# Head 0's first evictions by another engine, padded quarters, another order of the first two products, and two more products of zeros, in a two-layer graph attention kernel

## The chip, the cores and the metric

The kernel runs on one core of a Trainium2 chip. The time is that of the device, in microseconds, of one execution of the whole program. The engines have these names in the profile: PE is TensorE (PEld its weight loads), DVE is VectorE, ACT is ScalarE, POOL is GpSimd, SP is SyncE, which mostly issues DMAs. Each of them takes its instructions in order from a queue of its own and waits for the others by semaphores.

## The reference

A graph of 512 nodes has 16896 directed edges, sorted by destination: two times 8192 drawn ones and a loop at each node. Two layers of graph attention follow each other, the first with 8 heads, the second with one; all widths are 768. Then comes a residual and a layer norm.

```python
def gat_layer(x, W, a_s, a_d, b, edge_index, concat):
    n = x.shape[0]
    H, C = a_s.shape
    h = (x @ W).reshape(n, H, C)
    src, dst = (edge_index[0], edge_index[1])
    alpha_s = jnp.einsum('nhc,hc->nh', h, a_s)
    alpha_d = jnp.einsum('nhc,hc->nh', h, a_d)
    e = jax.nn.leaky_relu(alpha_s[src] + alpha_d[dst], NEG_SLOPE)
    m = jax.ops.segment_max(e, dst, num_segments=n)
    e = jnp.exp(e - m[dst])
    denom = jax.ops.segment_sum(e, dst, num_segments=n)
    alpha = e / (denom[dst] + EPS)
    msg = h[src] * alpha[:, :, None]
    out = jax.ops.segment_sum(msg, dst, num_segments=n)
    out = out.reshape(n, H * C) if concat else out.mean(axis=1)
    return out + b
h = jax.nn.elu(gat_layer(x, W1, a_src1, a_dst1, b1, edge_list, concat=True))
out = gat_layer(h, W2, a_src2, a_dst2, b2, edge_list, concat=True)
y = _layernorm(x + out)
```

## The kernel before

**Counts instead of edges.** The kernel turns the edge list into a dense matrix of counts, `cnt` (512 x 512: how many edges lead from a source to a destination), once, at the start. With it each head's attention is dense: logits for all pairs, a row maximum over existing edges, an exponential weighted by the counts, and a product with the features.

The 16896 edges are 132 chunks (`EC`) of 128 edges. For each chunk a one-hot of its sources (`os`, 128 x 512) is made, and TensorE multiplies it with a one-hot of its destinations (`od`), 32 nodes wide, and adds the product up in PSUM (L554, "counting"). Since the edges are sorted by destination, each chunk touches at most two blocks of 32 nodes, and these blocks are known in advance. `rel` (L265) is an edge's destination less the first node of either block. `destinations` (L507) compares `rel` with 0 to 31 (`offsets`) and so makes `od` for a quarter of the chunks, 33 of them, in one VectorE instruction; it rounds the quarter's bounds outwards to even columns, so that 34 columns are written. The comparisons come in the order of quarters 0, 2, 1, 3.

The one-hots of the sources are made by VectorE (L528, `is_equal`) or, for the destinations of the third quarter of nodes, by ScalarE (L526, `Sign`, from the negated index `nidx`, L611); they lie in 32 buffers that VectorE and ScalarE share in turn. Nine batches of 16 chunks (four in the last) are written out by hand: a batch makes its quarter's destinations if they are missing, its one-hots, then `extra` work, then a few of the items of the first projections (below), and then counts. `wants` says how many items are done by the end of each batch; evictions that VectorE has to do wait for the middle of the next batch's one-hots (`waiting`).

**Products by seven parts.** Each large fp32 product (512 x 768 by 768 x 768, or the aggregation) is split two by two and done with seven half-size products, P1 to P7 (a Strassen-like scheme), whose sums of operands are made by VectorE or by adding DMAs. A part has two row blocks (`i` = 0, 1) of 128 rows, and each has three contraction steps `k` of 128 (`product`, L305 to L310). The trace shows each such fp32 step as two records, so a row block is six.

`first_projection` is head 0's x times W1. Its P1 goes to two PSUM banks of the pool `held`; ScalarE copies them out (L430); later parts are added into the same banks. x is turned by TensorE (`turn_x(t, r)`, L213: three transposes of row tile t, column half r, into a bank of the pool `mm`, then a ScalarE copy to `xT`, L214). Half 0 of tiles 0 and 1 is turned ahead of everything; the rest comes between the items: `turns = {1: [(0, 1), (1, 1)], 3: [(2, 0), (3, 0), (2, 1), (3, 1)]}` says after how many items. After the first item `nidx` is made, and after each item some of the one-hots of ScalarE.

`keep_warm(n)` (L184) multiplies zeros, 128 x 128 by 128 x 512, n times, into a bank that nothing reads yet: five times at the very beginning, once after the first transposes.

**The heads.** For each head h the loop at L848 does the aggregation (`mixed`, L757, ends with ELU into `gT`), then `second`, head h's part of the second layer's projection (gT times a block of W2, added into `h2` and `u2`), with the next head's attention (`lift`, `leak`, `rank`, `weigh`) in between, and then `projection` of the head after next. In `second`, P2 is accumulated into P1's bank and P4 into P7's, P3 into P5's; between those the bank is evicted (`empty`, L362 to L367). For head 0 `h2` and `u2` are new, so the first eviction to each is a plain copy or negation by VectorE (L365); for the later heads it is an addition (L367). Around head 0's `second` the order is: both row blocks of P1; the eviction of block 0; the rest of the ELU; `gsums[0]`; the eviction of block 1; `gsums[1]`; a sum of W2; P2's blocks and the other sums; P2's evictions; then P6, P7, P4, P5, P3 with one tile of the attention beside each.

Of the kernel before, what the change touches and what calls it, by code (L numbers as in the profile page):

```python
# [8 lines left out]
F32 = mybir.dt.float32  # L9
F16 = mybir.dt.float16  # L10
BF16 = mybir.dt.bfloat16
# [3 lines left out]
ALU = mybir.AluOpType  # L15
# [21 lines left out]
def gat_pass(  # L37
# [16 lines left out]
    nc = tc.nc  # L54
# [127 lines left out]
    def keep_warm(n):  # L182
        for _ in range(n):
            nc.tensor.matmul(idle, zeros[:, :P], zeros, start=True, stop=True)  # L184

    keep_warm(5)
    nodes = ohp.tile([P, N], F16, name="nodes")
    nc.gpsimd.iota(nodes, pattern=[[1, N]], base=0, channel_multiplier=0,
                   allow_small_or_imprecise_dtypes=True)
# [30 lines left out]
    if general:  # L220
        nc.vector.tensor_copy(idx_f, idx_i)
        idx = ohp.tile([P, 2, EC], F32, name="idx")
        psi = tr.tile([P, 512], F32, name="tr")
        for j in range(2):
            for r in range(2):
                nc.tensor.transpose(psi[:, (2 * j + r) * EH:(2 * j + r + 1) * EH], idx_f[:, j, r, :],
                                    ident[:EH, :EH])
        nc.vector.tensor_copy(idx, psi[:, :2 * EC].rearrange("p (j c) -> p j c", j=2))
    else:

        B = 32
        blocks = []
        for c in range(EC):
            m = (c + 0.5) * P * N / E
            b = int(m // B)
            slack = 2 + 16 * (m / N * (1 - m / N)) ** 0.5
            lo, hi = b - (m - b * B < slack), b + ((b + 1) * B - m < slack)
            blocks.append(range(max(lo, 0), min(hi, N // B - 1) + 1))  # L240
        assert max(map(len, blocks)) <= 2


        base = ohp.tile([P, 2, EC], F32, name="base")
        for k in range(2):
            firsts = [b[k] if k < len(b) else None for b in blocks]
            lo = 0
            while lo < EC:
                hi = lo + 1
                while hi < EC and firsts[hi] == firsts[lo]:  # L250
                    hi += 1
                nc.gpsimd.memset(base[:, k, lo:hi], float(2 * N if firsts[lo] is None else firsts[lo] * B))
                lo = hi
        offsets = ohp.tile([P, B, 2, EC // NT + 1], F16, name="offsets")
        nc.vector.tensor_copy(offsets.rearrange("p b k c -> p b (k c)"),
                              nodes[:, :B].unsqueeze(2).to_broadcast([P, B, 2 * (EC // NT + 1)]))
        nc.vector.tensor_copy(idx_f, idx_i)
        turn_x(0, 0)
        turn_x(1, 0)
        psi = tr.tile([P, 512], F32, name="tr")  # L260
        for j in range(2):
            for r in range(2):
                nc.tensor.transpose(psi[:, j * EC + r * EH:j * EC + (r + 1) * EH], idx_f[:, j, r, :], ident[:EH, :EH])
        rel = ohp.tile([P, 2, EC], F16, name="rel")
        nc.vector.tensor_tensor(rel, psi[:, :EC].unsqueeze(1).to_broadcast([P, 2, EC]), base, op=ALU.subtract)  # L265
        idx = ohp.tile([P, EC], F32, name="idx")
        nc.vector.tensor_copy(idx, psi[:, EC:2 * EC])

# [83 lines left out]
    def second(h, A_, B_):  # L352

        bank = {}

        def pair(p, i, start, acc, new):
            def multiply(between=None):
                if start:
                    bank[i] = mm.tile([P, 512], F32, name="mm")
                product(bank[i], A_, B_, p, i, start, between)  # L360

            def empty():  # L362
                a, ps = acc(i), bank[i][:, :HALF]
                if new and (h == 0 or h == H - 1 and p == "P1"):
                    nc.vector.tensor_scalar(a, ps, -1.0 if p == "P7" else 1.0, None, op0=ALU.mult)  # L365
                else:
                    nc.vector.tensor_tensor(a, a, ps, op=ALU.subtract if p == "P7" else ALU.add)  # L367
            return multiply, empty

        steps = [  # L370
            ("P1", True, lambda i: u2[:, i, :], True),
            ("P2", False, lambda i: h2[:, i, L], True),
            ("P6", True, lambda i: u2[:, i, :], False),
            ("P7", True, lambda i: h2[:, 2 + i, R], True),
            ("P4", False, lambda i: h2[:, 2 + i, L], True),
            ("P5", True, lambda i: h2[:, 2 + i, R], False),
            ("P3", False, lambda i: h2[:, i, R], True),
        ]
        return [pair(p, i, *rest) for p, *rest in steps for i in range(2)]
# [29 lines left out]
        nc.vector.tensor_tensor(cnt[:, t, :], steps[:, 1:], steps[:, :N], op=ALU.subtract)  # L409
        nc.scalar.activation(absent[:, t, :], cnt[:, t, :], AF.Relu, bias=far, scale=NO_EDGE)  # L410

    def first_projection(h, XA, B_):


        HS[h] = hs = hpool.tile([P, NT, D], F32, name="hs")
        new_alpha(h)
        bank = {}

        def step(p, over, i, out, op):
            def multiply():  # L420
                if over is None:
                    bank[p, i] = (held if p == "P1" else mm).tile([P, 512], F32, name="held" if p == "P1" else "mm")
                else:
                    bank[p, i] = bank[over, i]
                product(bank[p, i], XA, B_, p, i, over is None)

            def empty():
                ps, o = bank[p, i][:, :HALF], out(i)
                if op is None:
                    nc.scalar.copy(o, ps)  # L430
                else:
                    nc.vector.tensor_tensor(o, o, ps, op=op)
            return multiply, empty, op is not None

        steps = [
            ("P1", None, lambda i: hs[:, i, L], None),
            ("P2", None, lambda i: hs[:, i, L], ALU.add),
            ("P5", None, lambda i: hs[:, 2 + i, R], None),
            ("P3", "P5", lambda i: hs[:, i, R], None),
            ("P6", "P1", lambda i: hs[:, i, R], ALU.subtract),  # L440
            ("P7", "P1", lambda i: hs[:, 2 + i, R], ALU.subtract),
            ("P4", "P1", lambda i: hs[:, 2 + i, L], None),
        ]
        return [step(p, over, i, out, op) for p, over, out, op in steps for i in range(2)]

    def spread(h):
        BC[h] = tr.tile([P, 512], F32, name="tr")
# [36 lines left out]
        nc.scalar.activation(nb1T, psb[:, :H * DC], AF.Copy, scale=-1.0)  # L484

    XA, xsums = left(xT, xS)
    items = first_projection(0, XA, B0)
    again = None
    if not general:

# [9 lines left out]
            hits[b] = hits.get(b, 0) + 1  # L500
        todo = dict(hits)
        cps, done = {}, set()
        od = ohp.tile([P, B, 2, EC], BF16, name="odw", bufs=1)

        def destinations(lo, hi):
            lo, hi = lo // 2 * 2, (hi + 1) // 2 * 2
            nc.vector.tensor_tensor(od[:, :, :, lo:hi], rel[:, :, lo:hi].unsqueeze(1).to_broadcast([P, B, 2, hi - lo]),  # L507
                                    offsets[:, :, :, :hi - lo], op=ALU.is_equal)

        def inside():  # L510

            below = ohp.tile([P, 2, EC], F16, name="below")
            nc.vector.tensor_scalar(below, rel, float(B), None, op0=ALU.is_lt)
            nc.vector.scalar_tensor_tensor(below, rel, 0.0, below, op0=ALU.is_ge, op1=ALU.mult, accum_out=found)

# [27 lines left out]
        def count(batch, rest):  # L543


            for c, b in ((c, b) for c in batch for b in blocks[c]):
                queues[b * B % P // B].append((c, b, hot[c, by_steps(b)]))
            while any(queues) and (rest or all(queues) or sum(map(len, queues)) > 3):
                for c, b, h_ in [q_.pop(0) for q_ in queues if q_]:
                    t, r = b * B // P, b * B % P  # L550
                    if t not in cps:
                        pool, name = (bc, "bc") if t == S else (tr, "tr")
                        cps[t] = pool.tile([P, 512], F32, name=name)
                    nc.tensor.matmul(cps[t][r:r + B, :N], od[:, :, b - blocks[c][0], c], h_,  # L554
                                     start=todo[b] == hits[b], stop=todo[b] == 1,
                                     tile_position=(0, r), skip_group_check=True)
                    todo[b] -= 1
            for t in range(NT):
                if t not in done and all(todo[b] == 0 for b in range(t * P // B, (t + 1) * P // B)):
                    (counted_by_steps if t == S else counted)(t, cps[t])  # L560
                    done.add(t)


        turns = {1: [(0, 1), (1, 1)], 3: [(2, 0), (3, 0), (2, 1), (3, 1)]}
        keep_warm(1)
        found = const.tile([P, 1], F32, name="found")
        wholes = len(items)
# [17 lines left out]
        pos, made, quarter, waiting = 0, set(), EC // NT, []  # L585
        for n, batch in enumerate(batches):
            for k in sorted({c // quarter for c in batch} - made):
                destinations(k * quarter, (k + 1) * quarter)
                made.add(k)
            sources(kinds(batch, False), waiting)  # L590
            ahead = kinds(batches[n + 1], True) if n + 1 < len(batches) else []
# [522 lines left out]
```

## Time and profile before

| | |
|---|---|
| three runs | 647.89, 647.94, 646.70 us (median 647.89) |
| the profiled execution | 647.22 us |
| its span, first to last instruction | 645.4 us |
| granted TensorE clock, mean | 0.998 |
| PE busy | 634.1 us (98%), 2327 matmul records |
| DVE busy | 517.4 us (80%) |
| ACT busy | 280.1 us (43%) |
| POOL busy | 46.1 us (7%) |
| DMA | 100.32 MB, mean 155 GB/s |

A profile shows one execution. A timeline row has the start and the duration in us, the engine, the line of the kernel, the operation, what it writes and reads, its shape and the number of instructions merged into the row; in brackets stand the idle time of the engine ahead of it and what ended that. The chain of waits is followed back from the last instruction: at each step to what released it, or to the instruction ahead of it on its engine. Busy PE is not PE at its peak, since matmuls are pipelined.

### The profile page before, as it was taken

What the parts mean: (1) busy time and instruction counts of PE and PEld (TensorE: products, weight loads), DVE (VectorE), ACT (ScalarE), POOL (GpSimd) and SP (SyncE); (2) the same over time, 40 slices, a digit from 0 to 9 for tenths busy, and PEclk for the clock granted to TensorE, in tenths of its full rate; (3) what the DMA queues carried; (4) which work ended last, traced back from release to release, by engine and by line L of the source; (5) the groups of instructions that cost most, each with busy time, mean ns of one, the idle gap of its engine ahead of it and who ended that gap; (6) DMA issues with size and microseconds to landing.
All of it is one profiled execution on the core that took longest, in us unless ns stands there. A gap on an engine that the chain in (4) does not pass through costs nothing.

```text
span 645.4 us, 7150 instructions
## 1 busy us (share of the span) xinstructions
PE 634.1 (98%) x2327; PEld 402.4 (62%) x2327; DVE 517.4 (80%) x1128; ACT 280.1 (43%) x472; POOL 46.1 (7%) x89
## 2 busy tenths in 40 slices
PE   8999999999999999999999999999999999999995
PEld 5555585556855586556855586556855586544553
DVE  8799989978689678878689678878689678876775
ACT  5865744530726035530726035530725035543440
POOL 1300011010000110011000110010000110000000
PEclk9999999999999999999999999999999999999999
DMA  8993488696715794196715794196815990410222
GB/s 297 326 230 87 74 248 270 151 256 193 188 55 135 187 257 139 27 259 187 188 56 134 188 258 138 29 258 193 185 54 139 233 258 16 107 50 0 30 60 77
DMA packets 81096, 100.32 MB, mean 155 GB/s; under 512 B 39654, under 2 KB 63006, under 8 KB 81054
## 3 DMA queue, kind: packets, MB, share of 16 engines
q1 hardware_dynamic: 67646, 78.57, 39.8%
q0 software_dynamic: 12976, 20.65, 18.4%
q10 hardware_dynamic: 432, 0.59, 0.3%
q8 instruction: 20, 0.33, 0.2%
q14 instruction: 22, 0.18, 0.1%
HBM read 86.93 MB, written 1.59 MB: 137 GB/s over the span
## 4 chain that ended last, share of the span: by engine, by line
PE 94%; DVE 4%; ACT 1%; DMA 1%; issue 0%; DVEq 0%; ACTq 0%
PE mm L309 62%; PE mm L779 20%; PE mm L725 3%; PE mm L1060 3%; PE held L309 2%; PE tr L554 1%; DVE os L528 1%; DMA hs<-in_x_dram 1%; PE mm L213 0%; PE bc L554 0%; DVE scr L318 0%; PE tr L984 0%; DVE h L365 0%; DVE q L475 0%; DVE q L470 0%
## 5 line engine op out<-in xcount | busy, mean ns | idle before, releaser
L309 PE MATMUL mm<-w,gT 128*128 128x384 f32 x288 | 96.8, 488 | 0.2 <-DVE u L365 0.2
L309 PE MATMUL mm<-w,xT 128*128 128x384 f32 x264 | 88.2, 487 | 0.0
L309 PEld LDWEIGHTS mm<-w,gT 128*128 128x128 f32 x288 | 54.3, 190 | 38.1 <-issue 1.6
L309 PEld LDWEIGHTS mm<-w,xT 128*128 128x128 f32 x264 | 49.9, 190 | 35.3 <-ACT os L526 0.8
L783 ACT COPY u<-mm 128x256 f32<-128x256 f32 x21 | 7.8, 372 | 140.5 <-PE mm L779 140.5
L477 ACT ACTIVATE q<-q,nmax 128x512 f32<-128x512 f32 x36 | 25.8, 721 | 95.4 <-DVE nmax L475 95.4
L779 PE MATMUL mm<-PT,hs 128*128 128x256 f32 x252 | 61.3, 379 | 0.0
L309 PE MATMUL mm<-w1t,gS 128*128 128x384 f32 x180 | 60.6, 486 | 0.0
L309 PE MATMUL mm<-w2t,xS 128*128 128x384 f32 x168 | 56.6, 487 | 0.0
L779 PEld LDWEIGHTS mm<-PT,hs 128*128 128x128 f32 x252 | 47.8, 190 | 8.4 <-issue 0.4
L309 PEld LDWEIGHTS mm<-w1t,gS 128*128 128x128 f32 x180 | 34.1, 190 | 24.2 <-issue 0.6
L367 DVE TENSOR_TENSOR h<-h,mm 128x384 f32<-128x384 f32 x72 | 39.1, 550 | 12.5 <-PE mm L309 12.0
L309 PEld LDWEIGHTS mm<-w2t,xS 128*128 128x128 f32 x168 | 31.8, 190 | 22.4 <-ACT q L466 0.4
L779 PE MATMUL mm<-pS,gS 128*128 128x256 f32 x168 | 43.2, 380 | 0.0
L707 ACT COPY PT<-zr 128x1024 uint16<-128x1024 uint16 x34 | 39.5, 1161 | 2.6 <-DMA zr<-pS 2.0
L779 PEld LDWEIGHTS mm<-pS,gS 128*128 128x128 f32 x168 | 31.8, 190 | 4.7 <-DVE pS L752 0.4
L702 ACT COPY pS<-q 128x1024 uint16<-128x1024 uint16 x26 | 27.2, 1045 | 16.6 <-DVE q L687 16.6
L309 PE MATMUL mm<-w1t,gT 128*128 128x384 f32 x96 | 32.4, 487 | 0.5 <-DVE h L365 0.5
L309 PE MATMUL mm<-w,gS 128*128 128x384 f32 x96 | 32.6, 486 | 0.0
L309 PE MATMUL mm<-w,xS 128*128 128x384 f32 x96 | 32.5, 487 | 0.0
L367 DVE TENSOR_TENSOR u<-u,mm 128x384 f32<-128x384 f32 x28 | 15.4, 553 | 18.8 <-PE mm L309 18.7
L108 POOL DMA_DIRECT2D w1t<-in_L_gnn_W_dram x7 | 8.9, 1267 | 302.3 <-DVE hs L742 173.5
(187 smaller groups left out, 1080.5 us busy)
## 6 DMA issues: line engine op xcount, KB each, us to landing
w<-in_L_gnn_W_dram SPq DMA_DIRECT2D x91, 384.0 KB
w<-in_L_gnn_W_dram POOLq DMA_DIRECT2D x16, 576.0 KB, 8.7
w2t<-in_L_gnn_W_dram SPq DMA_DIRECT2D x10, 576.0 KB
w1t<-in_L_gnn_W_dram SPq DMA_DIRECT2D x9, 576.0 KB
w2t<-in_L_gnn_W_dram POOLq DMA_DIRECT2D x8, 576.0 KB, 8.8
w1t<-in_L_gnn_W_dram POOLq DMA_DIRECT2D x7, 576.0 KB, 8.3
a_s<-in_L_gnn_a_src_dram SPq DMA_DIRECT2D x8, 384.0 KB
a_d<-in_L_gnn_a_dst_dram SPq DMA_DIRECT2D x8, 384.0 KB
```

Of the source, the lines that this page charges most:

```text
L108: nc.gpsimd.dma_start(t1, upper[:, :, R], accum_op=ALU.add)
L309: nc.tensor.matmul(ps[:, :HALF], A_[p][:, k, i * P:(i + 1) * P], B_[p][:, k, :], start=start and k == 0, stop=k == HK - 1, skip_group_chec ...
L367: nc.vector.tensor_tensor(a, a, ps, op=ALU.subtract if p == "P7" else ALU.add)
L477: nc.scalar.activation(q, q, AF.Exp, bias=nmax, scale=-1.0)
L528: nc.vector.tensor_scalar(o, nodes, idx[:, c:c + 1], None, op0=ALU.is_equal)
L554: nc.tensor.matmul(cps[t][r:r + B, :N], od[:, :, b - blocks[c][0], c], h_, start=todo[b] == hits[b], stop=todo[b] == 1, tile_position=(0, ...
L702: nc.scalar.copy(apart.rearrange("p (h n) -> p h n", h=2), q.bitcast(U16).rearrange("p (n h) -> p h n", h=2))
L707: nc.scalar.copy(PT.rearrange("p s n -> p (s n)").bitcast(U16).rearrange("p (s n h) -> p s n h", s=NT, h=2)[:, :, t * P:(t + 1) * P, :], p ...
L725: nc.tensor.matmul(ps[:, :N], HS[h][:, s, c * P:(c + 1) * P], PT[:, s, :], start=(s == 0), stop=(s == NT - 1))
L779: nc.tensor.matmul(bank[p][:, :HN], A_[p][:, k, c * P:(c + 1) * P], B_[p][:, k, :], start=over is None and k == 0, stop=k == 1, skip_group ...
L783: nc.scalar.copy(u, part("P1"))
L1060: nc.tensor.matmul(ps[:, :cols.stop - cols.start], PT[:, s, t * P:(t + 1) * P], h2[:, s, cols], start=(s == 2), stop=(s == 1))
```

## The change

1. `keep_warm(5)` becomes `keep_warm(7)`.
2. `rel`, `od`, `offsets` and `below` get a dimension for the quarters, each `QW` = 34 columns wide instead of sharing 132; the 34th column of `rel` is filled with -1 by GpSimd. `destinations` takes a quarter's number and writes that quarter alone.
3. In `second`, head 0's evictions of P1 and P2 are copies by ScalarE instead of multiplications by 1 on VectorE.
4. The first two items (P1 of head 0's projection, row blocks 0 and 1) become one: `firsts` does step k = 0 for both row blocks, step 1 for both, then `between()`, which turns half 1 of x's tiles 0 and 1, then step 2 for both. The second item's `multiply` does nothing; both evictions come after `firsts`, each at its old place.

```diff
-    keep_warm(5)
+    keep_warm(7)
...
+        QC = EC // NT
+        QW = QC + QC % 2
         base = ohp.tile([P, 2, EC], F32, name="base")
+        rel = ohp.tile([P, 2, NT, QW], F16, name="rel")
...
-        offsets = ohp.tile([P, B, 2, EC // NT + 1], F16, name="offsets")
+        if QW > QC:
+            nc.gpsimd.memset(rel[:, :, :, QC:], -1.0)
+        offsets = ohp.tile([P, B, 2, QW], F16, name="offsets")
...
-        rel = ohp.tile([P, 2, EC], F16, name="rel")
-        nc.vector.tensor_tensor(rel, psi[:, :EC].unsqueeze(1).to_broadcast([P, 2, EC]), base, op=ALU.subtract)
+        nc.vector.tensor_tensor(rel[:, :, :, :QC],
+                                psi[:, :EC].rearrange("p (q c) -> p q c", c=QC).unsqueeze(1).to_broadcast([P, 2, NT, QC]),
+                                base.rearrange("p k (q c) -> p k q c", c=QC), op=ALU.subtract)
...
             def empty():
                 a, ps = acc(i), bank[i][:, :HALF]
-                if new and (h == 0 or h == H - 1 and p == "P1"):
+                if new and h == 0 and p in ("P1", "P2"):
+                    nc.scalar.copy(a, ps)
+                elif new and (h == 0 or h == H - 1 and p == "P1"):
                     nc.vector.tensor_scalar(a, ps, -1.0 if p == "P7" else 1.0, None, op0=ALU.mult)
...
-    def first_projection(h, XA, B_):
+    def first_projection(h, XA, B_, between):
...
+        def firsts():
+            for k in range(HK):
+                if k == HK - 1:
+                    between()
+                for i in range(2):
+                    if k == 0:
+                        bank["P1", i] = held.tile([P, 512], F32, name="held")
+                    nc.tensor.matmul(bank["P1", i][:, :HALF], XA["P1"][:, k, i * P:(i + 1) * P], B_["P1"][:, k, :],
+                                     start=k == 0, stop=k == HK - 1, skip_group_check=True)
+
+        items = [step(p, over, i, out, op) for p, over, out, op in steps for i in range(2)]
+        for i, multiply in enumerate((firsts, lambda: None)):
+            items[i] = (multiply, *items[i][1:])
+        return items
...
+    def rest_of_x():
+        if not general:
+            for t in range(2):
+                turn_x(t, 1)
+
+    items = first_projection(0, XA, B0, rest_of_x)
...
-        od = ohp.tile([P, B, 2, EC], BF16, name="odw", bufs=1)
-
-        def destinations(lo, hi):
-            lo, hi = lo // 2 * 2, (hi + 1) // 2 * 2
-            nc.vector.tensor_tensor(od[:, :, :, lo:hi], rel[:, :, lo:hi].unsqueeze(1).to_broadcast([P, B, 2, hi - lo]),
-                                    offsets[:, :, :, :hi - lo], op=ALU.is_equal)
+        od = ohp.tile([P, B, 2, NT, QW], BF16, name="odw", bufs=1)
+
+        def destinations(q_):
+            nc.vector.tensor_tensor(od[:, :, :, q_, :], rel[:, :, q_, :].unsqueeze(1).to_broadcast([P, B, 2, QW]),
+                                    offsets, op=ALU.is_equal)
...
-        turns = {1: [(0, 1), (1, 1)], 3: [(2, 0), (3, 0), (2, 1), (3, 1)]}
+        turns = {3: [(2, 0), (3, 0), (2, 1), (3, 1)]}
```

More of the change, by code (lines that the diff above doesn't have):

```diff
@@ L253, in gat_pass @@
                 lo = hi
-        offsets = ohp.tile([P, B, 2, EC // NT + 1], F16, name="offsets")
+        if QW > QC:
+            nc.gpsimd.memset(rel[:, :, :, QC:], -1.0)
+        offsets = ohp.tile([P, B, 2, QW], F16, name="offsets")
         nc.vector.tensor_copy(offsets.rearrange("p b k c -> p b (k c)"),
-                              nodes[:, :B].unsqueeze(2).to_broadcast([P, B, 2 * (EC // NT + 1)]))
+                              nodes[:, :B].unsqueeze(2).to_broadcast([P, B, 2 * QW]))
         nc.vector.tensor_copy(idx_f, idx_i)
@@ L443, in first_projection @@
         ]
-        return [step(p, over, i, out, op) for p, over, out, op in steps for i in range(2)]
+        def firsts():
[11 more added lines that the diff above has]
+        return items
     def spread(h):
@@ L486, in gat_pass @@
     XA, xsums = left(xT, xS)
-    items = first_projection(0, XA, B0)
+    def rest_of_x():
[3 more added lines that the diff above has]
+    items = first_projection(0, XA, B0, rest_of_x)
     again = None
@@ L502, in gat_pass @@
         cps, done = {}, set()
-        od = ohp.tile([P, B, 2, EC], BF16, name="odw", bufs=1)
-        def destinations(lo, hi):
-            lo, hi = lo // 2 * 2, (hi + 1) // 2 * 2
-            nc.vector.tensor_tensor(od[:, :, :, lo:hi], rel[:, :, lo:hi].unsqueeze(1).to_broadcast([P, B, 2, hi - lo]),
-                                    offsets[:, :, :, :hi - lo], op=ALU.is_equal)
+        od = ohp.tile([P, B, 2, NT, QW], BF16, name="odw", bufs=1)
+        def destinations(q_):
+            nc.vector.tensor_tensor(od[:, :, :, q_, :], rel[:, :, q_, :].unsqueeze(1).to_broadcast([P, B, 2, QW]),
+                                    offsets, op=ALU.is_equal)
         def inside():
-            below = ohp.tile([P, 2, EC], F16, name="below")
+            below = ohp.tile([P, 2, NT, QW], F16, name="below")
             nc.vector.tensor_scalar(below, rel, float(B), None, op0=ALU.is_lt)
@@ L553, in count @@
                         cps[t] = pool.tile([P, 512], F32, name=name)
-                    nc.tensor.matmul(cps[t][r:r + B, :N], od[:, :, b - blocks[c][0], c], h_,
+                    nc.tensor.matmul(cps[t][r:r + B, :N], od[:, :, b - blocks[c][0], c // QC, c % QC], h_,
                                      start=todo[b] == hits[b], stop=todo[b] == 1,
@@ L587, in gat_pass @@
             for k in sorted({c // quarter for c in batch} - made):
-                destinations(k * quarter, (k + 1) * quarter)
+                destinations(k)
                 made.add(k)
```

## The prediction, made before the result was known

> **What bounds the kernel now.** I read the page's chain first, then the busy times by stage (columns: stretch, its length, then busy time and number of instructions of PE, PEld, DVE, ACT, POOL, then granted clock, DMA share, GB/s), then what TensorE waited for.
>
> ```profile
> PE 94%; DVE 4%; ACT 1%; DMA 1%; issue 0%; DVEq 0%; ACTq 0%
> ```
> ```profile
> 0.00:16.00 16.00, 13.57 (x52) 8.22 (x52) 12.96 (x39) 7.96 (x16) 2.88 (x54) 1.00 0.87 296
> ...
> 120.00:633.00 513.00, 512.97 (x1760) 328.85 (x1759) 405.36 (x850) 209.70 (x347) 30.43 (x24) 1.00 0.55 142
> ```
> ```profile
> PE held L309 <- DVE hs L432: 0.7, 2, 0.4
> ...
> PE mm L309 <- DVE h L365: 0.5, 1, 0.5
> ...
> PE mm L309 <- DVE u L365: 0.2, 1, 0.2
> ```
>
> TensorE carries the chain, and from 120 to 633 us it is busy for 512.97 of 513 us. So a microsecond that TensorE loses before 120 us goes straight into the end, and one saved there comes straight out. The diff touches only work before 120 us. The question is how much of the few waits above it takes away, and what it puts in their place.
>
> **The start: seven zeros products and the row blocks.** The timeline of the first 17 us (start, duration, engine and line, count, idle time before and what ended it):
>
> ```profile
> 1.28 2.31 PE L184 MATMUL bc<-zeros 128*128 128x512 bf16 x5 [1.28 <-DVE zeros L179]
> 4.38 1.51 PE L213 MATMUL mm<-ident,hs 128*128 128x128 f32 x6 [0.79 <-DMA hs<-in_x_dram]
> 5.29 0.48 ACT L214 COPY xT<-mm 128x384 f32<-128x384 f32 x1 [2.27 <-PE mm L213]
> 6.55 2.96 PE L309 MATMUL held<-w,xT 128*128 128x384 f32 x6
> 9.36 0.82 PE L213 MATMUL mm<-ident,hs 128*128 128x128 f32 x6
> 10.01 2.10 PE L309 MATMUL held<-w,xT 128*128 128x384 f32 x6
> 10.67 0.34 ACT L611 ACTIVATE nidx<-idx 128x132 f32<-128x132 f32 x1
> 11.11 1.33 ACT L526 ACTIVATE os<-nodes,nidx 128x512 bf16<-128x512 f16 x2
> 11.95 2.10 PE L309 MATMUL mm<-w,xT 128*128 128x384 f32 x6
> 12.35 0.46 ACT L430 COPY hs<-held 128x384 f32<-128x384 f32 x1
> 12.71 1.33 ACT L526 ACTIVATE os<-nodes,nidx 128x512 bf16<-128x512 f16 x2
> 14.41 0.86 ACT L214 COPY xT<-mm 128x384 f32<-128x384 f32 x2 [0.37 <-PE mm L213]
> 14.94 0.93 PE L213 MATMUL mm<-ident,hs 128*128 128x128 f32 x6 [0.24 <-ACT xT L214]
> 16.11 1.27 PE L554 MATMUL tr<-os,odw 128*32 128x512 bf16 x16
> ```
>
> Six transposes take 1.51 us at 4.38 and 0.82 at 9.36; the same product takes 2.96 us at 6.55 and 2.10 at 10.01. TensorE begins at half rate, though the granted clock reads 1.00 for the stretch. The excess of 0.86 us (2.96 - 2.10) is half of 1.72 us at half rate, so the full rate came at 6.55 + 1.72 = 8.27, that is 3.9 us after work resumed at 4.38. The earlier 2.31 us of zeros did not bring it, and then TensorE idled 0.79 us.
>
> Two more zeros products at 0.43 us (2.31 over five, less the tail) make 0.86 us and close this idle time, 0.07 over at worst; if x landed earlier, up to 0.8 would lie ahead of it. Counting 3.9 us from 1.28 then puts the full rate at 5.2 instead of 8.27. The Trainium skill (TensorE: Matmul & The Clock Gate, Part 1: The HAM clock gate) has a free-running window of about 3.4 us, at whose busy end the rate doubles: by it the switch moves one window earlier, to 4.9, and the sum would gain some 0.1 more. The trace's switch at 8.27 fits such a window; nothing in the rows shows its phase.
>
> With the full rate at 5.2, the first product starts when ScalarE has copied the first turned tile, 5.29 + 0.48 = 5.77, and has handed over (0.05 from the end of its copy at 14.41 + 0.48 to TensorE's start at 14.94, a little more with a weight load ahead): 5.9, not 6.55. By the starts 10.01 and 11.95 a product takes 1.94 us, a third of it 0.65. The new order does the first two thirds of both row blocks (2.58), then six transposes (0.65), then the last third of block 0, whose end drains for 0.16 (2.10 less 1.94): done at 5.9 + 2.58 + 0.65 + 0.65 + 0.16 = 9.94. Only then can ScalarE copy block 0, and its strict order puts behind that copy nidx, two one-hots, the copy of block 1, two more one-hots and the copy of x's third tile: 0.36 + 0.44 + 1.24 + 0.36 + 1.24 = 3.64 us by the starts 10.67, 11.11, 12.35, 12.71. That copy starts at 13.58, 0.8 before the 14.41 of now; TensorE waits for it at 14.94, and the counting behind follows. TensorE alone would have gained 1.5 (0.65 + 0.86). So here ScalarE becomes the late one, and the row-block order itself is a cost: there is no idle time between 6.55 and 11.95 that it could fill. If the rate does not rise earlier, block 0 is done at 11.95 - 0.65 + 0.16 = 11.46 and the copy starts at 15.10, 0.7 **later** than now. Term A: 0.8 gained, ends -0.7 and 1.5.
>
> **Padded quarters.** In before, quarter 1 of the one-hots (columns 33 to 65) is written as columns 32 to 65, so that it overwrites column 32 of quarter 0, which the counting of the third batch still reads. This is the wait:
>
> ```profile
> 13.01 1.29 DVE L507 TENSOR_TENSOR odw<-rel,offsets 128x2176 bf16<-128x2176 f16 x1
> ...
> 28.69 1.29 DVE L507 TENSOR_TENSOR odw<-rel,offsets 128x2176 bf16<-128x2176 f16 x1 [4.30 <-PE tr L554]
> 29.90 3.87 DVE L528 TENSOR_SCALAR os<-nodes,idx 128x512 bf16<-128x512 f16 x12
> 33.68 0.95 DVE L291 TENSOR_TENSOR xT<-xT 128x768 f32<-128x768 f32 x1
> 34.55 1.66 DVE L528 TENSOR_SCALAR os<-nodes,idx 128x512 bf16<-128x512 f16 x6
> 36.13 1.01 DVE L432 TENSOR_TENSOR hs<-hs,held 128x384 f32<-128x384 f32 x2
> 36.73 4.14 PE L309 MATMUL held<-w,xT 128*128 128x384 f32 x12 [0.44 <-DVE hs L432]
> ...
> 42.14 4.14 PE L309 MATMUL held<-w1t,xT 128*128 128x384 f32 x12 [0.25 <-DVE hs L432]
> ```
>
> VectorE stands for 4.30 us, then works without a break until the eviction at 36.13, for which TensorE waits 0.44. With quarters of their own the comparison starts at about 24.4. Of the twelve one-hots behind it some seven reuse buffers that are already read; the rest waits for the third batch's counting, which ends just before 28.69. So VectorE is some 3 us ahead at 36.13, and the 0.44 goes. The 0.25 at 42.14 stays: the eviction there lies behind a one-hot whose buffer the fifth batch's counting must first release, right before. Instruction sizes stay (2176 elements: 34 columns now too); one POOL memset more meets an engine that is busy for 2.88 of the first 16 us. Term B: 0.44, ends 0 and 0.69.
>
> What is late next is an addition by DMA, into W1's upper right, which the product at 36.73 reads:
>
> ```profile
> 19.70 1.62 POOL L385 DMA_DIRECT2D w<-in_L_gnn_W_dram x1
> ```
> ```profile
> w<-in_L_gnn_W_dram POOLq DMA_DIRECT2D x1, 576.0 KB, 14.5
> ```
>
> It lands at 19.70 + 14.5 = 34.2; TensorE would want it 1.2 us earlier than 36.73, at 35.5. 1.3 us are left.
>
> **The four copies by ScalarE.** P2 adds into P1's bank, P4 into P7's, so both need the eviction before:
>
> ```profile
> 102.66 4.29 PE L309 MATMUL mm<-w,gT 128*128 128x384 f32 x12
> 104.14 0.55 DVE L365 TENSOR_SCALAR u<-mm 128x384 f32<-128x384 f32 x1
> 106.53 0.55 DVE L365 TENSOR_SCALAR u<-mm 128x384 f32<-128x384 f32 x1
> 107.14 2.20 PE L309 MATMUL mm<-w,gT 128*128 128x384 f32 x6 [0.19 <-DVE u L365]
> 112.14 1.02 DVE L365 TENSOR_SCALAR h<-mm 128x384 f32<-128x384 f32 x2
> 114.53 0.72 ACT L477 ACTIVATE q<-q,nmax 128x512 f32<-128x512 f32 x1 [10.27 <-DVE nmax L475]
> 117.24 1.02 DVE L365 TENSOR_SCALAR h<-mm 128x384 f32<-128x384 f32 x2
> 117.84 4.14 PE L309 MATMUL mm<-w1t,gT 128*128 128x384 f32 x12 [0.50 <-DVE h L365]
> ```
>
> From 102.66 to 117.84 lie seven products of six records, 7 x 1.94 = 13.6 us of work in 15.18: 1.6 us lost, of which the waits name 0.69 (0.19 + 0.50). VectorE loses four evictions of 0.47 (1.02 for two, less 0.55), 1.9 us, ahead of the one at 117.24. ScalarE takes 0.46 per copy (row 12.35) and idles 10.27 us here: both copies of P1 end within 0.6 us of their products, so P2 no longer waits. The first eviction of P7 could come at 115.4, while TensorE has P7's second block until 102.66 + 13.6 = 116.2, so P4 follows P7 directly. What moves: the lift of q's first tile now stands behind four copies, at 102.66 + 3 x 1.94 + 0.16 + 0.46 = 109.1; VectorE wants it at 112.14 + 1.02 - 1.9 = 111.3. Term C: 1.5, a little under the whole loss, ends 0.69 and 1.6; a loss is excluded by the 10.27 us of idle ScalarE.
>
> **Sum.** 0.8 + 0.44 + 1.5 = 2.7 us. The profiled execution took 647.22 us (span 645.4), 0.67 below the median of 647.89: 644.5 against its own time, 645.2 against the median, which I take. A measurement of this kernel can tell about 0.2%, 1.3 us, from no change.
>
> **Rivals.**
> - *The rate does not rise earlier* (0.17). For: 2.31 us of zeros left no mark, and transposes follow the zeros directly. Then A is -0.7, the sum 1.24, the time 646.7: within 0.2%. Against: it rose at 8.27 with transposes at the head of the busy stretch. The Trainium skill (same page, Part 4: PE-mode transpose) says that transposes do not count as busy; by it zeros alone would have to bring the rate. The trace speaks against it: of the 3.9 us from 4.38 to 8.27 the first 1.51 were transposes.
> - *Slower: the quarters still count as overlapping* (0.07), since they interleave in memory. Every later comparison would then wait for the counting before it. The second, now right behind the first batch's one-hots, would stand from 13.01 - 0.65 = 12.4 until the first counting's end at 17.38 - 0.8 = 16.6, and all that VectorE does behind it would be 4.2 late, 3.5 against now. The fourth would wait for the fifth batch's counting, with no cover left: its own 1.29 and the 0.44 of the eviction behind. 3.5 + 1.7 - 1.5 (C) = 3.7 slower, 651.6. It decides once the second stands for about 2 us. Against: the comparison at 13.01 writes columns that interleave with quarter 0 in just this way, ahead of the counting at 16.11 that reads those, and did not wait.
> - *A wait that I don't see takes 1.3 us or more* (0.09), the DMA addition above before all: by its margin of 1.3 us it costs nothing until it lands later than 35.5; landing 2 us later than now it would leave a gain of 2.0.
>
> **How the numbers follow.** Forecast 0.67. Low end: the fastest run, 646.70, less 2.9. High end: the first rival at 646.7 and a little for its spread, 647.0. Faster by over 0.2%: the forecast and part of the rest, 0.7. Within: 0.17. Slower: 0.13.
>
> **What would show it.** Zeros without a gap until 4.3, the first product at 5.9 with all its records at the full rate, ScalarE's third x copy at 13.6; the wait of 4.30 before the comparison gone and TensorE's wait at 36 with it; P4 of head 0's second product right behind P7, at 2.7 us earlier than 117.84. A first product still at 6.55 refutes A; a comparison that waits for L554 refutes B; TensorE waiting for ScalarE near 104 refutes C.

## The result, and the profile after

Six runs of the changed kernel have a median of 644.46 us (644.03 to 645.04), six of the kernel before 647.84 (646.70 to 648.00): the ratio is 0.9957, with an interval of 0.9944 to 0.9971, so 1.9 to 3.6 us faster. The profiled execution took 644.97 us (span 643.2), 2.25 less than that of before. The forecast was 645.2, and 2.7 less.

The busy times by stage show where the 2.2 us of span lie. The stretches are cut at the same events in both kernels: first counting, fifth counting, start of head 0's second product, its P4, start of the next aggregation, end. Columns as above. First the kernel before, then the changed one:

```profile
0.00:16.07 16.07, 13.58 (x54) 8.23 (x56) 13.03 (x39) 8.03 (x16) 2.88 (x54) 1.00 0.87 297
16.07:40.79 24.72, 24.28 (x151) 13.28 (x151) 20.35 (x54) 19.55 (x36) 5.92 (x5) 1.00 1.08 302
40.79:100.72 59.93, 58.97 (x287) 37.94 (x287) 54.91 (x143) 35.42 (x62) 4.30 (x4) 1.00 0.59 139
100.72:117.84 17.12, 16.41 (x49) 8.68 (x47) 16.28 (x29) 5.29 (x10) 2.53 (x2) 1.00 1.06 326
117.84:156.65 38.81, 38.81 (x121) 22.91 (x121) 31.47 (x64) 13.17 (x17) 2.53 (x2) 1.00 0.69 167
156.65:645.40 488.75, 482.04 (x1671) 311.39 (x1669) 381.38 (x803) 198.67 (x335) 27.89 (x22) 1.00 0.53 139
```
```profile
0.00:15.89 15.89, 13.48 (x55) 8.46 (x56) 13.07 (x39) 8.01 (x16) 2.95 (x55) 1.00 0.89 294
15.89:40.11 24.22, 24.22 (x152) 13.31 (x152) 20.96 (x55) 19.05 (x35) 5.91 (x5) 1.00 1.08 303
40.11:100.03 59.92, 58.96 (x287) 37.95 (x287) 54.38 (x141) 35.93 (x63) 4.36 (x4) 1.00 0.60 142
100.03:115.63 15.60, 15.60 (x50) 9.03 (x48) 14.46 (x24) 7.31 (x15) 2.53 (x2) 1.00 1.05 331
115.63:154.33 38.70, 38.70 (x122) 22.80 (x120) 31.59 (x64) 12.95 (x17) 2.53 (x2) 1.00 0.74 178
154.33:643.20 488.87, 482.04 (x1671) 311.40 (x1669) 381.36 (x803) 198.66 (x335) 27.89 (x22) 1.00 0.52 139
```

The start gained 0.18 us, the counting 0.50, the second product 1.52, what follows it 0.11, and the rest nothing. The last stretch is the same to 0.12 us: what was won early arrived at the end.

The start, from the timeline of the changed kernel:

```profile
1.28 3.17 PE L184 MATMUL bc<-zeros 128*128 128x512 bf16 x7 [1.28 <-DVE zeros L179]
4.24 1.49 PE L213 MATMUL mm<-ident,hs 128*128 128x128 f32 x6
6.38 2.91 PE L460 MATMUL held<-w,xT 128*128 128x384 f32 x8
9.79 1.46 PE L460 MATMUL held<-w,xT 128*128 128x384 f32 x4
10.63 0.48 ACT L438 COPY hs<-held 128x384 f32<-128x384 f32 x1
11.42 1.33 ACT L552 ACTIVATE os<-nodes,nidx 128x512 bf16<-128x512 f16 x2
12.66 0.46 ACT L438 COPY hs<-held 128x384 f32<-128x384 f32 x1
13.02 1.33 ACT L552 ACTIVATE os<-nodes,nidx 128x512 bf16<-128x512 f16 x2
14.26 0.84 ACT L214 COPY xT<-mm 128x384 f32<-128x384 f32 x2
14.77 0.93 PE L213 MATMUL mm<-ident,hs 128*128 128x128 f32 x6 [0.94 <-ACT xT L214]
```

The seven zeros products close the gap ahead of x. The six transposes behind them still take 1.49 us, where six at the full rate take 0.82, so they run at half rate. The first product's eight records at 6.38 come at the full rate but for a part of the first. ScalarE's third x copy follows its one-hots without idle time (before it had idled 0.37 there), and TensorE waits 0.94 us for it.

The counting, same view:

```profile
24.15 1.28 DVE L533 TENSOR_TENSOR odw<-rel,offsets 128x2176 bf16<-128x2176 f16 x1
25.36 3.24 DVE L554 TENSOR_SCALAR os<-nodes,idx 128x512 bf16<-128x512 f16 x12
34.55 0.55 DVE L440 TENSOR_TENSOR hs<-hs,held 128x384 f32<-128x384 f32 x1 [1.38 <-PE held L315]
36.04 4.14 PE L315 MATMUL held<-w,xT 128*128 128x384 f32 x12
...
40.58 0.35 DVE L554 TENSOR_SCALAR os<-nodes,idx 128x512 bf16<-128x512 f16 x1 [1.38 <-PE tr L580]
```

The third comparison waits for nothing. VectorE now waits for TensorE ahead of the evictions, and TensorE's product at 36.04 for nobody. So the DMA addition into W1, which the prediction named as the next possible wait, costs nothing here: it was issued at 19.54 and landed 14.5 us later, at 34.0. The one-hot at 40.58 waits for the fifth batch's counting, and the eviction behind it costs TensorE 0.25 us as before.

The second product:

```profile
100.03 7.90 PE L315 MATMUL mm<-w,gT 128*128 128x384 f32 x24
102.86 0.46 ACT L371 COPY u<-mm 128x384 f32<-128x384 f32 x1
104.11 0.48 ACT L371 COPY u<-mm 128x384 f32<-128x384 f32 x1 [0.79 <-PE mm L315]
107.78 4.14 PE L315 MATMUL mm<-w1t,gS 128*128 128x384 f32 x12
107.97 0.48 ACT L371 COPY h<-mm 128x384 f32<-128x384 f32 x1 [1.46 <-PE mm L315]
108.35 0.72 ACT L488 ACTIVATE q<-q,al_d 128x512 f32<-128x512 f32 x1
110.65 0.69 DVE L492 SCALAR_TENSOR_TENSOR q<-q 128x512 f32<-128x512 f32 x1
114.82 0.55 DVE L373 TENSOR_SCALAR h<-mm 128x384 f32<-128x384 f32 x1
115.63 4.03 PE L315 MATMUL mm<-w1t,gT 128*128 128x384 f32 x12
```

TensorE goes through P1, P2, P6, P7 and P4 without a wait. ScalarE's copies follow their products, and it has idle time ahead of three of the four.

### The profile page after: what moved, and what is told of

Same layout as the page of the kernel before. It is cut to its first block, busy times and chain, and to the rows that moved or that the text cites. A ratio compares the mean times of both kernels' runs of the same rounds, so it can differ in the third digit from the quotient of the medians.

```text
span 643.2 us, 7161 instructions
## 1 busy us (share of the span) xinstructions
PE 633.0 (98%) x2329; PEld 403.0 (63%) x2329; DVE 515.8 (80%) x1124; ACT 281.9 (44%) x476; POOL 46.2 (7%) x90
## 4 chain that ended last, share of the span: by engine, by line
PE 97%; ACT 1%; DVE 1%; issue 0%; DVEq 0%; ACTq 0%
PE mm L315 65%; PE mm L805 20%; PE mm L751 3%; PE mm L1086 3%; PE held L315 2%; PE tr L580 1%; PE bc L184 1%; PE held L460 1%; PE bc L580 0%; ACT os L552 0%; PE mm L213 0%; PE tr L1010 0%; DVE os L554 0%; PE tr L719 0%; ACT xT L214 0%
```

## The experiments

Each kernel was timed beside the kernel before in five rounds, in three groups; the kernels of a group share a chip, and each group has another one; that of the result above is not known. The first four each make one part of the change on the kernel before.

**Zeros alone.**

```diff
-    keep_warm(5)
+    keep_warm(7)
```

> Only the two more zeros products, on the kernel before. Theory (closing TensorE's idle time brings the full rate one window earlier, whatever the window's phase): the full rate comes between 4.7 and 7.9 us instead of after 7.8; in the old order ScalarE is not late, so TensorE's whole gain counts: 1.0 to 1.5 us faster than before. Rival (the rate rises at a time of its own, and the 6.7 us of the changed kernel was another phase, not the zeros): within 0.3 us of before.

Ratio 0.9998 (0.9988 to 1.0008): the rival's case. The trace has the first counting at 14.69 us, 1.4 before that of the kernel before in its profile, but the other three kernels of this group, with five zeros products, are early too (14.61, 14.63, 15.11). And a part of the lead was lost again: the twelve one-hots behind the third comparison take 4.27 us instead of 3.87, and TensorE waits longer for the eviction behind them:

```profile
28.52 4.27 DVE L528 TENSOR_SCALAR os<-nodes,idx 128x512 bf16<-128x512 f16 x12
```
```profile
PE held L309 <- DVE hs L432: 1.1, 2, 0.9
```

From first to fifth counting this kernel needs 25.14 us, the one before 24.72, the changed one 24.22. What makes these one-hots slower is not shown; over the four kernels without padding their time does not follow the lead (see the part on why the prediction was right).

**ScalarE's copies alone.**

```diff
-                if new and (h == 0 or h == H - 1 and p == "P1"):
+                if new and h == 0 and p in ("P1", "P2"):
+                    nc.scalar.copy(a, ps)
+                elif new and (h == 0 or h == H - 1 and p == "P1"):
```

> Only head 0's evictions of P1 and P2 by ScalarE, on the kernel before. Theory: 1.5 us faster, P1, P2, P6, P7, P4 of head 0's second product without idle time between them. Rival (the wait at P4 was that of the attention beside it, or the gain needs VectorE's lead from the padded quarters): 0.2 to 0.7 us, a wait for VectorE left at P4.

Ratio 0.9987 (0.9974 to 1.0000): 0.8 us, 0 to 1.7, which does not tell the theory's 1.5 from the rival's 0.2 to 0.7. The trace does, and shows the theory's case: the second product begins at 99.38 us and P4 at 114.98, so 15.60 us as in the changed kernel, without the quarters. No wait for VectorE is left at P4.

```profile
107.13 4.14 PE L309 MATMUL mm<-w1t,gS 128*128 128x384 f32 x12
111.11 4.03 PE L309 MATMUL mm<-w,gT 128*128 128x384 f32 x12
114.98 1.45 PE L309 MATMUL mm<-w1t,gT 128*128 128x384 f32 x4
```

**Padded quarters alone** (`rel`, `od`, `offsets`, `below` and `destinations` as in the change, the rest as before).

> Only the padded quarters, on the kernel before. Theory: the wait of 4.30 us ahead of the third comparison is gone, TensorE's wait of 0.44 us at the eviction near 36 us too: 0.5 us faster. Rival (VectorE's work is late at the fifth batch again, by the one-hot buffers): below 0.2 us, TensorE's wait near 42 us longer by as much.

The trace shows the edit at work: the comparison starts without a wait, and first to fifth counting takes 24.21 us.

```profile
23.89 1.29 DVE L512 TENSOR_TENSOR odw<-rel,offsets 128x2176 bf16<-128x2176 f16 x1
25.10 3.24 DVE L533 TENSOR_SCALAR os<-nodes,idx 128x512 bf16<-128x512 f16 x12
```

The times show no gain: ratio 0.9999 (0.9987 to 1.0010), which excludes more than 0.8 us of gain. 0.5 us is inside it; that the stretch's 0.5 to 0.9 us reached the end in every run is not shown.

**Row blocks alone** (`firsts` and `between` as in the change, the rest as before).

> Only the row-block order of the first two products, on the kernel before. Theory (the order delays ScalarE's copy of the first block and with it the copies of x behind it): 0.7 us slower, TensorE waits for ScalarE's third x copy for about 0.9 us instead of 0.24. Rival (the order is neutral: what limits there is TensorE or the landing of x): within 0.2 us of before, no longer wait for ScalarE.

Ratio 1.0012 (1.0001 to 1.0023): 0.8 us **slower**, and the place is the one named.

```profile
11.87 0.46 ACT L430 COPY hs<-held 128x384 f32<-128x384 f32 x1
12.23 1.33 ACT L544 ACTIVATE os<-nodes,nidx 128x512 bf16<-128x512 f16 x2
13.47 0.84 ACT L214 COPY xT<-mm 128x384 f32<-128x384 f32 x2
```
```profile
13.98 0.93 PE L213 MATMUL mm<-ident,hs 128*128 128x128 f32 x6 [0.68 <-ACT xT L214]
```

The four ratios multiplied give 0.9996, 0.3 us, far less than the whole change. The times of single parts hold the start, which moves from run to run. Counted in the profiles from the first counting to the end, the start is left out, and the parts add up: 629.4 us before, 629.6 with zeros alone, 629.5 with row blocks alone, 628.9 with quarters alone, 627.7 with ScalarE's copies alone, and 627.0 to 627.4 in the seven profiles of this document that have copies and quarters together and keep the sixth batch's evictions at their place.

**The second group** has the changed kernel again and three that tell its parts apart.

> The changed kernel once more, beside the three that follow on the same chip. Theory (the parts add by stretches of the timeline: start to first counting, first to fifth counting, head 0's second product): second product 1.6 us, first to fifth counting 0.5 to 0.9, less some 0.7 for the row-block order; the zeros give nothing where x lands before 3.9 us and up to 1.5 where it lands after 4.3: 1.4 to 1.9 us faster than before with an early x, 2.2 to 3.4 with a late one. Rival (the zeros carry the change on every chip): over 2.5 us in either case.

0.9969 (0.9958 to 0.9979): 2.0 us faster on this chip, between the two ranges of the theory. In its trace x starts at 4.20, between the two cases as well. Over 2.5, the rival's case, lies in the interval only at the edge.

Without row blocks:

```diff
-    items = first_projection(0, XA, B0, rest_of_x)
+    items = first_projection(0, XA, B0)
...
-        turns = {3: [(2, 0), (3, 0), (2, 1), (3, 1)]}
+        turns = {1: [(0, 1), (1, 1)], 3: [(2, 0), (3, 0), (2, 1), (3, 1)]}
```

> The changed kernel with the first two products in their old order. Theory (the row-block order delays ScalarE's first copy and what stands behind it): 0.5 to 0.8 us faster than the changed kernel; TensorE's wait for ScalarE's x copy back at 0.24 us. Rival (the row blocks help once the full rate comes early, by covering the landing of W1 and x): 0.2 us or more slower than the changed kernel, waits for DMA in the first product.

0.9962 (0.9947 to 0.9976), 0.5 us better than the changed kernel beside it, in the forecast direction but within the intervals. TensorE's wait for ScalarE's x copy is back at 0.24 us.

Copies and quarters alone (the kernel above with `keep_warm(5)`):

> ScalarE copies and padded quarters alone: five zeros products, the old order. Theory: equal to the one without row blocks within 0.3 us where x lands before 3.9 us, up to 1.5 us slower where it lands later. Rival (closing the gap always brings the rate a window earlier): 0.8 us or more slower than the one without row blocks.

0.9965 (0.9953 to 0.9977), equal to the kernel with seven. In its trace x starts at 3.90 us, after 0.30 us of idle time. On this chip two of the four parts make the whole gain.

ScalarE's one-hots early:

```diff
     def rest_of_x():
         if not general:
+            early_ones()
             for t in range(2):
                 turn_x(t, 1)
...
+        def early_ones():
+            nc.scalar.activation(nidx, idx, AF.Copy, bias=0.5, scale=-1.0)
+            for c in ahead[:2 * share]:
+                one_hot(c, True)
+            del ahead[:2 * share]
...
-                if pos == 1:
-                    nc.scalar.activation(nidx, idx, AF.Copy, bias=0.5, scale=-1.0)
-                for c in ahead[:share]:
-                    one_hot(c, True)
-                del ahead[:share]
+                if pos > 2:
+                    for c in ahead[:share]:
+                        one_hot(c, True)
+                    del ahead[:share]
```

> The changed kernel, with nidx and four of ScalarE's one-hots ahead of its copies of x's second half (in the row-block order ScalarE idles there for some 3 us). Theory (what the row-block order costs is ScalarE's order): TensorE's wait for the third x copy goes, 0.7 to 1.2 us faster than the changed kernel, and no slower than the one without row blocks. Rival (x's last tile, the landing of which comes near 12.7 us, takes the place of ScalarE): below 0.3 us.

0.9962 (0.9949 to 0.9975), median 643.65 beside 644.14: 0.5 us, short of the theory's 0.7 and above the rival's 0.3, and no slower than the kernel without row blocks. The trace shows the wait for ScalarE back at its old 0.24, with the row blocks still there; ScalarE has time to spare ahead of the third copy:

```profile
7.16 2.56 ACT L553 ACTIVATE os<-nodes,nidx 128x512 bf16<-128x512 f16 x4
9.63 0.83 ACT L214 COPY xT<-mm 128x384 f32<-128x384 f32 x2
10.36 0.88 ACT L438 COPY hs<-held 128x384 f32<-128x384 f32 x2
13.02 0.86 ACT L214 COPY xT<-mm 128x384 f32<-128x384 f32 x2 [1.78 <-PE mm L213]
```
```profile
13.55 0.93 PE L213 MATMUL mm<-ident,hs 128*128 128x128 f32 x6 [0.24 <-ACT xT L214]
```

**The third group: fewer zeros, and the best version.** Five (`keep_warm(5)` in the changed kernel):

> The changed kernel with the five zeros products of before. Theory (a stretch with less than about 80% of TensorE's time busy does not bring the full rate; the stretch's phase differs from run to run): with x landing at 3.6 to 3.9 us the idle time is 0.25 to 0.5 us and costs nothing, so within 0.3 us of the changed kernel's ratio to before (0.997); where x lands after 4.3, up to 1.5 us slower. Rival (two zeros products more always pay): 0.8 us or more slower in either case.

Three (`keep_warm(3)`):

> The changed kernel with three zeros products: TensorE idles 1.1 to 1.4 us ahead of x. Theory: that stretch no longer counts as busy, the full rate comes between 6.6 and 10 us, 1.0 to 1.5 us slower than with five zeros products, and at half rate the first product's records show it. Rival (the rate rises at a time of its own): within 0.3 us of five.

Five give 0.9976 (0.9964 to 0.9988). That is 0.5 us behind the changed kernel's 0.9969 and 1.2 behind its 0.9957, neither of them measured beside it; in the profile x starts late, at 4.39, for which the theory allows up to 1.5, so theory and rival are not told apart. Three give 0.9987 (0.9977 to 0.9997): 0.7 us behind five by the ratios, 0.5 by the medians, with intervals that overlap. It is the direction of the theory, below its 1.0 to 1.5, and not clear of the rival's 0.3. The two profiles differ in x's landing too:

```profile
4.39 1.51 PE L213 MATMUL mm<-ident,hs 128*128 128x128 f32 x6 [0.80 <-DMA hs<-in_x_dram]
6.57 2.65 PE L460 MATMUL held<-w,xT 128*128 128x384 f32 x6
```
```profile
4.02 1.51 PE L213 MATMUL mm<-ident,hs 128*128 128x128 f32 x6 [1.27 <-DMA hs<-in_x_dram]
6.19 3.23 PE L460 MATMUL held<-w,xT 128*128 128x384 f32 x6
```

The kernel that takes what the others pointed to, on top of the early one-hots:

```diff
-    keep_warm(7)
+    keep_warm(6)
...
-                if j == len(chunks) // 2:
+                if j == (5 if n == 5 else len(chunks) // 2):
```

> The changed kernel with nidx and four of ScalarE's one-hots early, six zeros products, and in the sixth batch the two evictions one one-hot earlier, ahead of the one-hot that waits for the fifth batch's counting. Theory: the cost of the row blocks (0.7) and TensorE's wait of 0.25 us near 41 us go, and x waits for no zeros: 0.9 to 1.3 us faster than the changed kernel, 2.9 us or more faster than before. Rival (the evictions wait for the products in any case, and move the one-hots behind them): the wait near 41 stays or grows, 0.6 us or less.

0.9954 (0.9939 to 0.9969), median 643.93 beside 646.64 for before: 2.0 to 3.9 us faster, as forecast against before (2.9 or more) and the best ratio of all, though its interval overlaps that of the changed kernel. Beside the changed kernel with five zeros products, on the same chip, it is 1.3 us lower in the median (643.93 to 645.25); what six zeros products and what the early evictions add to this, the times don't tell. TensorE no longer waits near 41 us: the second eviction comes right behind its product, and the product that needs it follows the counting.

```profile
39.67 0.55 DVE L440 TENSOR_TENSOR hs<-hs,held 128x384 f32<-128x384 f32 x1 [0.56 <-PE held L315]
40.58 2.85 PE L315 MATMUL held<-w1t,xT 128*128 128x384 f32 x8
```

**One reading of all thirteen profiles.** The full rate's time is the start of the trace's record of the granted clock, which has no entry before the first grant of the full clock. At the same place the starts of single records change their spacing, from 0.43 to 0.22 us (zeros), 0.21 to 0.11 (transposes) or 0.64 to 0.32 (products). The excess is what the first product's records lost at half rate. The last column is the first counting less the first product's start and less the excess.

| kernel | zeros products | x starts | full rate from | first product | excess | first counting | rest |
|---|---|---|---|---|---|---|---|
| before | 5 | 4.38 | 8.3 | 6.55 | 0.86 | 16.07 | 8.66 |
| changed | 7 | 4.24 | 6.7 | 6.38 | 0.16 | 15.90 | 9.36 |
| zeros alone | 7 | 4.24 | 5.5 | 6.05 | 0 | 14.69 | 8.64 |
| copies alone | 5 | 3.61 | 5.7 | 5.96 | 0 | 14.61 | 8.65 |
| quarters alone | 5 | 3.90 | 5.8 | 5.98 | 0 | 14.63 | 8.65 |
| row blocks alone | 5 | 3.93 | 5.2 | 5.76 | 0 | 15.11 | 9.35 |
| changed, again | 7 | 4.20 | 4.0 | 5.72 | 0 | 15.07 | 9.35 |
| no row blocks | 7 | 4.24 | 7.3 | 6.39 | 0.46 | 15.50 | 8.65 |
| copies and quarters | 5 | 3.90 | 6.9 | 6.12 | 0.39 | 15.15 | 8.64 |
| early one-hots | 7 | 4.24 | 5.2 | 6.03 | 0 | 14.68 | 8.65 |
| five zeros | 5 | 4.39 | 7.7 | 6.57 | 0.56 | 16.46 | 9.33 |
| three zeros | 3 | 4.02 | 8.5 | 6.19 | 1.14 | 16.66 | 9.33 |
| early, six zeros | 6 | 3.96 | 7.3 | 6.13 | 0.57 | 15.34 | 8.64 |

The rest takes two values only: 8.65 without row blocks or with the one-hots early, 9.35 with row blocks. The row-block order costs 0.70 us in every profile that has it with ScalarE's one-hots at their old place, and since it costs nothing with the one-hots early, ScalarE's order is its whole cost. The full rate comes anywhere between 4.0 and 8.5 us: with seven zeros products at 4.0 to 7.3 (mean 5.7 of five profiles), with five at 5.2 to 8.3 (mean 6.6 of six). The two overlap too much for one profile of each kernel to tell them apart. Seven zeros products also hold TensorE until 4.24, past the 3.61 to 3.93 at which x started in four of the profiles with five.

## Why the prediction was right, and where it was not

*ScalarE's copies (term C, 1.5).* 1.52 in the profiles: up to P4 the second product takes 15.60 us, within 0.01, in all nine profiles with ScalarE's copies, and 17.12 in all four without, whatever else is changed. The side steps held too: the lift of q moved to 108.35 (109.1 had been worked out on the old time axis, which lies 0.7 later), and VectorE took it up at 110.65 without having waited.

*Padded quarters (term B, 0.44).* 0.50: the wait of 4.30 is gone and with it the one at 36; that of 0.25 near 41 stayed, for the reason given, which the last kernel shows by moving the eviction ahead of the one-hot. What I missed is that the twelve one-hots behind the late comparison also take longer, and not equally long: 3.87 us before, 3.99, 4.18 and 4.27 with copies, row blocks and zeros alone, against 3.24 in the padded kernels of the first two groups. The wait at the eviction follows them (0.44, 0.57, 0.77, 0.86), so that B is worth 0.5 to 0.9. It does not follow the start, though the latest start has the least: the first countings of these four lie at 16.07, 14.61, 15.11 and 14.69. The rival in which quarters still count as overlapping is refuted: no comparison waits.

*Zeros and row blocks (term A, 0.8).* This is the step that failed: 0.18 in the profiles, and what failed in it is the time of the full rate. Its second half, ScalarE's order, was right to the hundredth: from ScalarE's copy of block 0 to the third x copy 3.64 us were counted, and 3.63 passed (10.63 to 14.26); the cost of the row blocks, put at 0.7 by the case without an earlier rate, is 0.70. Its first half was not: "counting 3.9 us from 1.28 puts the full rate at 5.2" took one interval of one execution for a property. The full rate came at 6.7, 5.4 us after the first zeros product; the first rival, by which it would not come earlier than 8.3, did not hold either. So the first product started at 6.38 rather than 5.9, and A is the smaller excess (0.86 to 0.16, 0.70) and the earlier start (0.17), less the 0.70 of the row blocks: 0.17.

The traces also show what lies behind the 3.9 us. The full clock, once granted, lasts 634.88 us in eight of the thirteen profiles and 631.47 in the other five, 186 and 185 times 3.413 us. So it is granted and withdrawn in steps of 3.41 us, while the first zeros product starts at 1.28 in all of them: where the steps fall differs between executions. In all thirteen, the 3.41 us that end at the full rate hold 0.80 or more of busy TensorE, the 3.41 us before them 0.77 or less. In the kernel before, the step from 1.47 to 4.88 held the idle time ahead of x (0.77 busy), and the full rate came one step later, at 8.29. In the changed kernel a step ended at 3.30 and had the time up to 1.28 idle in it, and the next one ended at 6.71. By this an idle time ahead of x matters only where it falls into the step that decides; that is an argument from the traces, since no run sets where the steps fall.

That the zeros caused even this excess to shrink is not shown. Zeros alone changed no time that could be measured (0.9998), seven and five did equally well on one chip (0.9962, 0.9965), and the table has late full rates with seven and early ones with five. The Trainium skill's free-running window (TensorE: Matmul & The Clock Gate, Part 1: The HAM clock gate) fits a time that differs by 2.7 us from run to run with the same kernel (6.7 and 4.0 for the changed one); its "±500ns run-to-run" does not. What remains open is a kernel whose x lands late on the same chip with and without the gap; the third group comes nearest to it, with 0.7 us between three and five zeros products and intervals that overlap, and five behind the changed kernel's earlier ratios by 0.5 to 1.2.

*The sum* came out near the measured one partly by luck: 2.25 us in the profiles for 2.7, with A 0.6 short and the other terms as forecast. In the medians the gain is larger, 3.4 us, since the profiled execution of before lies 0.6 below its median and that of the changed kernel 0.5 above; in the second group the gain was 2.0 by the ratio. The part of it that the profiles show each time is the 2.0 us of B and C. The start differs by 0.8 us between two executions of the changed kernel (first counting at 15.90 and 15.07) and by 1.5 among kernels whose code is the same up to there (16.07 before, 14.61 with copies alone), which could account for the rest; whether it did in those runs is not shown, because the timed runs have no profile.

## What to carry to other kernels

An eviction that the matrix engine waits for is worth moving to an engine that is idle at that moment, and the gain can be counted from product starts rather than from the named waits, which held less than half of it here (0.69 of 1.52). Rounding a slice outwards may overwrite a neighbour that is still being read; padding the layout removed the wait here, and the comparison took no longer (1.28 us for 1.29). Reordering work on one engine moves what the others may start: what stands behind the first delayed copy in its engine's strict order has to be counted, or moved ahead of it.

## What the runs showed of the hardware that was not expected

TensorE's first microseconds run at half rate until a moment that lay between 4.0 and 8.5 us over thirteen profiles. The granted clock reads 1.00 for these stretches in both kernels' rows above, because its record begins only with the first grant; the spacing of equal records shows the half rate. In one kernel the moment moved by 2.7 us between two executions, and the full clock lasts a whole number of steps of 3.413 us in all thirteen.

The landing of x moved as well: with the same five zeros products TensorE idled between nothing (x at 3.61) and 0.80 us ahead of it. One profile each is not enough to compare two kernels' starts. Behind the start the profiles repeat better: among kernels with the same code there, the stretches up to P4 of the second product agree to 0.03 us, but for the counting without padding (24.72 to 25.14). What follows P4 differs by up to 0.3 us.
